# A two-layer diffusion transformer in fp32 on one core: order of the first loads and products, place of the modulations, order at phase borders

## The chip, the cores and the metric

The kernel runs on one core of a Trainium2 chip. The metric is the time of one execution on the device in microseconds (us). The engines named below are PE (TensorE, matrix products, with PEld for its weight loads), DVE (VectorE), ACT (ScalarE), POOL (GpSimd) and SP (SyncE, which issues the transfers, DMAs). Each engine takes its instructions in the order of the program; an instruction that waits holds everything behind it on its engine. All DMAs of this kernel are issued from SP's queue.

## What is computed

The input x holds 16 samples of 256 tokens with 256 features; cond is one vector of 256 features for each sample, ctx a context of 256 tokens with 192 features. Two layers follow each other, and each has three phases: self-attention, cross-attention on the context, and a feed-forward network (FFN). All is fp32.

```python
# layer 0: adaln(x) = ln(x, w, b) * (1 + cond @ g_w + g_b) + cond @ b_w + b_b
x = x + attn(adaln1(x), adaln1(x))            # 16 heads of 64, rotary positions
x = x + attn(adaln1(x), ln(ctx))              # the same modulation 1
x = x + gelu(adaln2(x) @ w1 + b1) @ w2 + b2
# layer 1: (sh1, sc1, sh2, sc2, sh3, sc3) = silu(cond) @ Wmod + bmod
x = x + attn(ln1(x) * (1 + sc1) + sh1) @ Wos + bos          # 16 heads of 16
x = x + attn(ln2(x) * (1 + sc2) + sh2, ctx) @ Woc + boc
x = x + gelu((ln3(x) * (1 + sc3) + sh3) @ W1 + b1) @ W2 + b2
```

## The kernel before

The program goes through the six phases one after the other, and in each phase through the 16 samples. A pair of phase and sample is a *job*; an attention job has two steps, an FFN job four. The loop over the list `steps` writes the work of all engines out in order: in the step of one job it also issues pieces of its neighbours (`prev`, `nxt`, `after`, `third` are the jobs one behind and one, two and three ahead). `tc.manual_schedule` keeps that order; before, it is entered only when the loads of phase 0 and the first modulation have been issued, and what stands ahead of it is ordered by the framework. The eight PSUM banks are given out by hand; in the FFN `next_bank()` goes round them.

*Products.* `product` (L82) makes four column tiles of 32 that run side by side. Each fp32 product is two PE instructions.

*Modulation.* `modulation` makes `factor` and `addend` for all samples of a phase from two 256x256 matrices: 8 products of 16 columns, so 16 PE instructions (L152), and on DVE four small operations for each half of the features (L158 to L161). Layer 0 has two modulations (the first also serves the cross-attention), layer 1 has three. `load_phase` loads a phase's modulation matrices (L139, L140) and weights while the first job of the phase before runs; the modulation itself is made in job 2 of the phase before.

*Attention input.* `prepare_moments` makes the statistics (DVE, and POOL for the power, L261), `prepare_norm` normalizes and turns blocks of 32 by 32 (DVE), writes them to HBM by four DMAs (`turned`, L284) and adds the output bias to x on POOL (`add_bias`, L354). `prepare_fetch` reads them back by four DMAs (`fetched`, L294), and `prepare_input` makes hT from them, one half on ACT (L327), one on POOL (L328). For the very first job PE makes the transposition instead (L803).

*Layer 0's attention.* `stage_rotary` makes queries and keys of two heads' halves, DVE multiplies them by the rotary table (L455), POOL adds or subtracts (qk, L463). `stage_s` makes the scores (L498) and ACT their exponentials (pr, L510). `stage_t`, `stage_turn` and `stage_reduce` sum them on DVE into `rows`; `layer0_values` (PE, then ACT copies, L407) makes the values, `layer0_sums` (L567) the weighted sums. `sum_up` takes the sums of a whole job with one small product, inverts them on DVE (L541), writes them to HBM and spreads them back by one and four DMAs (L544, L547). `scale` multiplies the weighted sums by them on POOL (L556, four operations). `finish` makes the output product and adds it to x on DVE (L704).

*Layer 1's attention.* `stage_a` makes queries and keys, `layer1_values` the values (DVE writes them, L418), `layer1_sums` the weighted sums (L583), `normalize` inverts (L609), shuffles and multiplies (DVE, POOL, L618).

*FFN.* `ffn_hidden` makes a quarter of the hidden features in a step, ACT applies gelu (L633). The second product is made in Strassen's way: `fold_weights` makes five sums of quarters of w2, `fold_hidden` five of the hidden features (both DVE), and `finish_folded` makes seven products of quarters and adds them to x by five DVE operations. The last job of a phase uses `finish` instead, which makes the whole product.

At the border from layer 0's cross-attention to the FFN, three of these chains end behind each other: the next-to-last job's `scale` and `finish`, and the last job's `sum_up`, `scale` and `finish`, which come in the FFN's first two jobs:

```python
                if s == 2 and prev["kind"] == "attn":
                    (sum_up if prev["layer"] == 0 else finish)(prev, next_bank())
                if late is not None and s == 0:
                    scale(late)
                if late is not None and s == 3:
                    finish(late, next_bank())
```

Of the kernel before, what the change touches and what calls it, by code (L numbers as in the profile page):

```python
# [10 lines left out]
F32 = mybir.dt.float32  # L11
# [5 lines left out]
P = 128  # L17
# [26 lines left out]
def fast(ctx: ExitStack, tc: tile.TileContext, a: dict, out: bass.AP, flag):  # L44
# [6 lines left out]
    assert NB >= 5  # L51
# [19 lines left out]
    turn_of_ffn = [0]  # L71
# [12 lines left out]

    ident = work.tile([P, P], F32, tag="ctx", name="ident")
# [36 lines left out]

    sig = work.tile([NB, D], F32, tag="inv", name="sig")
    nc.scalar.activation(sig, cond, AF.Sigmoid)
    silu = work.tile([NB, D], F32, tag="inv", name="silu")
    nc.vector.tensor_mul(silu, sig, cond)
    condT = const.tile([P, 2, KC, NB], F32, name="condT")
    pc = bank(5, 2 * KC, NB).rearrange("p (s c) b -> p s c b", s=2)
    for s, src in enumerate((cond, silu)):
        for c in range(KC):  # L130
            nc.tensor.transpose(pc[:, s, c, :], src[:, c * P : (c + 1) * P], ident[:NB, :NB])
    nc.vector.tensor_copy(condT, pc)
    pr = bank(6, n_rows)
    nc.tensor.transpose(pr, rows, ident[:n_rows, :n_rows])
    nc.vector.tensor_copy(cols, pr)
# [7 lines left out]
    def modulation(name, at, which, w, ln_w, ln_b, shift_b, scale_b):  # L143


        factor = stat.tile([P, KC, NB], F32, tag="fac", name=f"fac_{name}", bufs=3)
        addend = stat.tile([P, KC, NB], F32, tag="add", name=f"add_{name}", bufs=3)
# [8 lines left out]
        for m in range(KC):  # L156
            one = stat.tile([P, NB], F32, tag="one", name=f"one_{name}_{m}", bufs=2)
            nc.vector.tensor_scalar(one, pm[:, 1, m, :], scale_b(m), 1.0, ALU.add, ALU.add)  # L158
            nc.vector.tensor_scalar(factor[:, m, :], one, ln_w(m), None, ALU.mult)
            nc.vector.tensor_scalar(one, one, ln_b(m), None, ALU.mult)  # L160
            nc.vector.scalar_tensor_tensor(addend[:, m, :], pm[:, 0, m, :], shift_b(m), one, ALU.add, ALU.add)  # L161
        return factor, addend

    def layer0_modulation(i):
        w = load_modulation(a[f"L0_xcond_b{i}_w"], a[f"L0_xcond_g{i}_w"], f"a{i}")
        return lambda at: modulation(
            f"a{i}", at, 0, w,
            lambda m: column(f"L0_xcond_ln{i}_w", m), lambda m: column(f"L0_xcond_ln{i}_b", m),
            lambda m: column(f"L0_xcond_b{i}_b", m), lambda m: column(f"L0_xcond_g{i}_b", m),
        )  # L170

    def layer1_modulation(i):
# [4 lines left out]
        c = at // P  # L177
        return lambda at: modulation(
            f"b{i}", at, 1, w,
# [1366 lines left out]
```

## Time and profile before

| | us |
|---|---|
| three runs | 2239.78, 2242.82, 2244.06 (median 2242.82) |
| the profiled execution | 2240.03, its span 2238.2 |
| PE busy in the span | 2208.3 |
| DVE, ACT, POOL busy | 1583.4, 837.1, 866.2 |
| first product of a whole stage (values of job 0) | starts at 12.32 |
| last addition to x, then its DMA out | 2231.88, 2232.60 |

The phases stand in the span about like this: self-attention of layer 0 to 674, its cross-attention to 1309, its FFN to 1542, self-attention of layer 1 to 1776, its cross-attention to 2010, its FFN to the end. A row of the timeline gives start, time, engine, line, operation, what is written and read, how often, and in brackets how long the engine was idle before and what ended that. A row that says x32 covers 32 instructions from the start of the first to the end of the last. A row of the waits names the engine that waited, what it was to run, whom it waited for, and then the total, how often, and the longest. The engine called SPq is SP's queue.

### The profile page before, as it was taken

Reading aid. Unit: us, or ns where it says so; the run is one execution under the profiler, and the core shown is the slowest. Engines: PE = TensorE matmul, PEld = TensorE weight load, DVE = VectorE, ACT = ScalarE, POOL = GpSimd, SP = SyncE. Lnnn points to the kernel's source line nnn. Section 1 sums busy time; section 2 is a strip of 40 time slices with the busy share of each in tenths; the row PEclk is TensorE's granted clock in tenths of the full one; section 3 lists DMA queues with packets and bytes.
Section 4 is the critical chain, followed back from the end, with each engine's and each line's share of the span. In section 5 each row is a group of like instructions: output and inputs, shape, how many; then the busy total and the mean of one; then the engine's idle time right before and its main releaser. Section 6 shows DMA issues by size and latency. Waiting matters only on the chain.

```text
span 2238.2 us, 104439 instructions
## 1 busy us (share of the span) xinstructions
PE 2208.3 (99%) x47515; PEld 1365.8 (61%) x47515; DVE 1583.4 (71%) x3001; ACT 837.1 (37%) x1302; POOL 866.2 (39%) x873
## 2 busy tenths in 40 slices
PE   8999999999999999999999999999999999999998
PEld 4555555555555555555555557876566555656786
DVE  5777677677678787887878775564777777777663
ACT  2233233233233332333333232223666656663322
POOL 3444444444445455554554532211222322322220
PEclk9999999999999999999999999999999999999999
DMA  8111111011123221222212122222111232223221
GB/s 249 39 27 35 22 27 36 22 27 36 25 46 80 62 54 37 45 53 42 56 35 55 27 50 74 41 46 60 41 42 40 52 101 61 60 51 78 65 62 36
DMA packets 305678, 117.29 MB, mean 52 GB/s; under 512 B 242548, under 2 KB 288968, under 8 KB 305096
## 3 DMA queue, kind: packets, MB, share of 16 engines
q1 hardware_dynamic: 305224, 110.51, 20.7%
q8 instruction: 374, 6.13, 1.2%
q14 instruction: 80, 0.66, 0.1%
HBM read 77.14 MB, written 33.29 MB: 49 GB/s over the span
## 4 chain that ended last, share of the span: by engine, by line
PE 93%; DVE 2%; DMA 1%; POOL 1%; SPq 1%; issue 1%; ACT 0%; POOLq 0%; DVEq 0%; ACTq 0%
PE banks L82 60%; PE banks L498 15%; PE banks L567 9%; PE banks L583 5%; PE banks L434 2%; PE banks L402 1%; DMA wkv_sa<-in_sa_wkv 1%; POOL raw L556 0%; DVE m L455 0%; POOL qk L463 0%; DMA spread<-sums_seen 0%; SPq L284 0%; PE banks L152 0%; DMA every<-sums_seen 0%; DMA x<-in_x 0%
## 5 line engine op out<-in xcount | busy, mean ns | idle before, releaser
L510 ACT ACTIVATE pr<-banks 128x1024 f32<-128x1024 f32 x576 | 487.5, 937 | 222.8 <-PE banks L498 194.6
L463 POOL TENSOR_TENSOR qk<-m,m 128x512 f32<-128x512 f32 x256 | 340.9, 1352 | 341.0 <-DVE m L455 230.8
L455 DVE TENSOR_TENSOR m<-banks,rope 128x512 f32<-128x512 f32 x512 | 325.2, 681 | 92.8 <-POOL qk L463 57.2
L519 DVE TENSOR_TENSOR both<-pr 128x512 f32<-128x512 f32 x256 | 217.8, 860 | 72.7 <-ACT pr L510 70.6
L574 ACT COPY raw<-banks 128x512 f32<-128x512 f32 x128 | 75.0, 587 | 469.9 <-PE banks L567 389.3
L498 PE MATMUL banks<-qk 32*64 32x256 f32 x8192 | 238.5, 377 | 1.0 <-DVE inv L541 0.5
L567 PE MATMUL banks<-pr,v 128*32 128x256 f32 x4096 | 233.5, 379 | 1.5 <-ACT pr L510 1.2
L498 PEld LDWEIGHTS banks<-qk 32*64 32x64 f32 x8192 | 184.4, 131 | 78.4 <-issue 53.0
L633 ACT ACTIVATE g<-banks,cols 128x256 f32<-128x256 f32 x256 | 107.0, 472 | 283.4 <-PE banks L82 270.5
L407 ACT COPY v<-banks 128x512 f32<-128x512 f32 x128 | 71.9, 588 | 357.6 <-PE banks L82 178.9
L556 POOL TENSOR_TENSOR raw<-raw,spread 128x512 f32<-128x512 f32 x128 | 182.4, 1457 | 27.8 <-DMA spread<-sums_seen 27.3
L567 PEld LDWEIGHTS banks<-pr,v 128*32 128x32 f32 x4096 | 130.2, 110 | 84.7 <-ACT pr L510 1.7
L704 DVE TENSOR_TENSOR x<-banks,x 128x512 f32<-128x512 f32 x66 | 45.6, 691 | 165.8 <-PE banks L82 165.8
L525 DVE STREAM_TRANSPOSE squares<-both 128x1024 f32<-128x1024 f32 x128 | 159.1, 1243 | 3.3
L532 DVE TENSOR_REDUCE rows<-squares 128x32 f32<-128x1024 f32 x128 | 154.0, 1203 | 2.2
L261 POOL TENSOR_TENSOR rstd<-ve,neg_half 128x2 f32<-128x2 f32 x95 | 67.5, 710 | 205.8 <-DVE ve L259 202.4
L82 PE MATMUL banks<-hT,wkv_sa 128*32 128x256 f32 x2048 | 136.1, 380 | 0.0
L583 PE MATMUL banks<-pr,wide_v 128*32 128x256 f32 x2048 | 134.4, 379 | 1.1 <-ACT pr L510 1.1
L82 PE MATMUL banks<-hT,wq_sa 128*32 128x256 f32 x2048 | 135.1, 379 | 0.0
L82 PE MATMUL banks<-hT,wq_ca 128*32 128x256 f32 x2048 | 134.0, 379 | 0.0
L498 PE MATMUL banks<-q,k 32*64 32x256 f32 x4096 | 129.2, 382 | 2.5 <-DVE add_b L161 2.1
L618 POOL TENSOR_TENSOR oT<-oT,spread 128x256 f32<-128x256 f32 x64 | 45.8, 737 | 210.7 <-DVE spread L617 210.7
(142 smaller groups left out, 3473.0 us busy)
## 6 DMA issues: line engine op xcount, KB each, us to landing
turned<-blocks SPq DMA_DIRECT2D x380, 64.0 KB
fetched<-turned SPq DMA_DIRECT2D x380, 64.0 KB
spread<-sums_seen SPq DMA_DIRECT2D x128, 128.0 KB
x<-in_x SPq DMA_DIRECT2D x16, 256.0 KB
fetched_c<-turned_c SPq DMA_DIRECT2D x64, 64.0 KB
cT<-in_ctx_turned SPq DMA_DIRECT2D x16, 256.0 KB
out<-x SPq DMA_DIRECT2D x16, 256.0 KB
ctx<-in_ctx SPq DMA_DIRECT2D x16, 192.0 KB
```

The lines of the kernel that those rows point to most:

```text
L82: nc.tensor.matmul(out[cut], lhsT[:, cut], rhs, start=start, stop=stop)
L455: nc.vector.tensor_tensor(m, pq, rope[:, s : s + 1, :].to_broadcast([P, 2, N]), ALU.mult)
L463: nc.gpsimd.tensor_tensor(r, x, y, (ALU.subtract, ALU.add)[out])
L498: nc.tensor.matmul(banks[64 * g : 64 * g + 64, at + h, t * N : (t + 1) * N], lhs, rhs, start=(half == 0), stop=(half == 1 or job["layer"] ...
L510: nc.scalar.activation(pr[:, one], sc[:, one], AF.Exp, scale=0.125 if job["layer"] == 0 else 0.25)
L519: nc.vector.tensor_tensor(job["both"][:, 2 * p : 2 * p + 2, :], pr[:, :, 0, :], pr[:, :, 1, :], ALU.add)
L525: nc.vector.transpose(job["squares"].rearrange("p b k -> p (b k)"), job.pop("both").rearrange("p h n -> p (h n)"))
L532: nc.vector.tensor_reduce(job["rows"][:, u, :], job.pop("squares"), AX.X, ALU.add)
L556: nc.gpsimd.tensor_tensor(part, part, spread[:, u : u + 1, :].to_broadcast([P, 2, N]), ALU.mult)
L567: nc.tensor.matmul(o[32 * h : 32 * h + 32, half, :], v[:, t, col : col + 32], prs[h // 2][:, h % 2, t, :], start=(t == 0), stop=(t == NT - 1),
L583: nc.tensor.matmul(o[32 * h : 32 * h + 32], v[:, t, 4 * c + h, 32 * e : 32 * e + 32], prs[h // 2][:, h % 2, t, :], start=(t == 0), stop=(t ...
L633: nc.scalar.activation(g[:, c, :], ph[:, c, :], AF.Gelu, bias=column(w["b1"], 2 * u + c))
```

## The change

*The start.* The whole program now stands in the order in which it is written. The first loads go out in another order: behind the modulation's matrices come the first halves of keys' and queries' weights, rope, the values' weights, fold, mask and the next two samples, then the other halves, the bias and wo. Twenty idle products of 16 columns, whose result nobody reads, are put between the transpositions of cond, of silu and of the vectors, and behind them; a one-column Exp is put behind the Sigmoid. The first modulation is made ahead of the transposition of the normalized x. All four rotary pieces of job 0 come ahead of both value steps, and the preparations of jobs 1 and 2 are placed anew.

*Modulations.* `modulation` has five DVE operations over both halves instead of eight. The three modulations of layer 1 are loaded and made in layer 0's FFN, in its jobs 2, 5 and 8.

*Borders.* At the last step of layer 0's attention other banks are used for the sums and for `finish`. In layer 0's FFN `sum_up` moves one step ahead, `scale` from the second job's first step to the first job's last; in layer 1's FFN `finish` moves behind the hidden product; `fold_weights` moves from the fourth step to the second. The values of layer 1's first job get a bank for each half. At the last step of layer 1's attention `finish` goes ahead of the sums. The turn of the FFN's banks starts one later.

*The end.* The last job uses `fold_hidden` and `finish_folded` as well, with an order of its own and a third bank.

The diff, without changes of indentation; the quoted keys in `phases` and the passing of columns are left out:

```diff
-    turn_of_ffn = [0]
+    turn_of_ffn = [1]
...
+    ctx.enter_context(tc.manual_schedule(engines={
+        mybir.EngineType.PE, mybir.EngineType.DVE, mybir.EngineType.Activation, mybir.EngineType.Pool,
+        mybir.EngineType.SP,
+    }))
     ident = work.tile([P, P], F32, tag="ctx", name="ident")
...
+    def transpose_condition(s, src):
+        pc = bank(5 + s, KC, NB)
+        for c in range(KC):
+            nc.tensor.transpose(pc[:, c, :], src[:, c * P : (c + 1) * P], ident[:NB, :NB])
+        nc.vector.tensor_copy(condT[:, s], pc)
+
+    def idle_products(n):
+
+        for _ in range(n):
+            nc.tensor.matmul(bank(0, 16), ident, ident[:, 0:16], start=True, stop=True)
+
     nc.scalar.activation(sig, cond, AF.Sigmoid)
+    soon = stat.tile([NB, 1], F32, tag="ve", name="soon")
+    nc.scalar.activation(soon, cond[:, 0:1], AF.Exp)
     silu = work.tile([NB, D], F32, tag="inv", name="silu")
+    idle_products(5)
+    transpose_condition(0, cond)
     nc.vector.tensor_mul(silu, sig, cond)
-    for s, src in enumerate((cond, silu)):
-        for c in range(KC):
-            nc.tensor.transpose(pc[:, s, c, :], src[:, c * P : (c + 1) * P], ident[:NB, :NB])
-    nc.vector.tensor_copy(condT, pc)
-    pr = bank(6, n_rows)
+    idle_products(4)
+    transpose_condition(1, silu)
+    idle_products(5)
+    pr = bank(4, n_rows)
     nc.tensor.transpose(pr, rows, ident[:n_rows, :n_rows])
-    nc.vector.tensor_copy(cols, pr)
+    idle_products(6)
...
-        for m in range(KC):
-            one = stat.tile([P, NB], F32, tag="one", name=f"one_{name}_{m}", bufs=2)
-            nc.vector.tensor_scalar(one, pm[:, 1, m, :], scale_b(m), 1.0, ALU.add, ALU.add)
-            nc.vector.tensor_scalar(factor[:, m, :], one, ln_w(m), None, ALU.mult)
-            nc.vector.tensor_scalar(one, one, ln_b(m), None, ALU.mult)
-            nc.vector.scalar_tensor_tensor(addend[:, m, :], pm[:, 0, m, :], shift_b(m), one, ALU.add, ALU.add)
+        nc.vector.tensor_tensor(addend, pm[:, 1], scale_b, ALU.add)
+        nc.vector.scalar_tensor_tensor(factor, addend, 1.0, ln_w, ALU.add, ALU.mult)
+        nc.vector.scalar_tensor_tensor(addend, addend, 1.0, ln_b, ALU.add, ALU.mult)
+        nc.vector.tensor_tensor(addend, addend, shift_b, ALU.add)
+        nc.vector.tensor_tensor(addend, pm[:, 0], addend, ALU.add)
...
+        load_keys(halves[0])
+        load_queries(halves[0])
+        if between is not None:
+            between(0)
+        load_keys(halves[2])
+        load_keys(halves[3])
+        if between is not None:
+            between(1)
+        load_queries(halves[1])
+        load_keys(halves[1])
+        bo = broadcast_row(a[f"L0_xcond_{kind}_bo"], "bo", f"bo_{kind}")
         nc.sync.dma_start(out=wo, in_=chunked(a[f"{kind}_wo"]))
...
+        if job is jobs[-1]:
+            sums = sums[4:] + sums[:4]
...
+        third = bank(next_bank(), 4, P) if final else second
...
+        for m in (3, 6, 4, 5, 2, 1, 7) if final else places:
             for c in range(4):
-                product(place, hidden[m][:, c, :], weights[m][:, c, :], c == 0, c == 3)
+                product(places[m], hidden[m][:, c, :], weights[m][:, c, :], c == 0, c == 3)
...
-    for dst, name in ((rope, "rope"), (fold, "fold"), (mask, "mask")):
-        nc.sync.dma_start(out=dst, in_=a[name])
-    for b in range(1, NB):
+    for b in range(3, NB):
         load_x(b)
-    phases[0]["mod"] = phases[0]["make_mod"](4)
...
-    xh = normalized(xs[0], moments(xs[0], "first"), D, "first")
+    found = moments(xs[0], "first")
+    nc.vector.tensor_copy(cols, pr)
+    xh = normalized(xs[0], found, D, "first")
+    phases[0]["mod"] = phases[0]["make_mod"](3)
...
     prepare_input(jobs[0])
-    add_bias(jobs[0])
-    layer0_values(jobs[0], 0)
     for e in range(2):
         for half in range(2):
             rotary((jobs[0], 0), e, half)
-    layer0_values(jobs[0], 1)
+        if e == 0:
+            prepare_moments(jobs[1])
+    for t in range(NT):
+        layer0_values(jobs[0], t)
     scores(0)
-    for job in jobs[1:3]:
-        prepare_moments(job)
-        prepare_norm(job)
+    prepare_norm(jobs[1])
     prepare_fetch(jobs[1])
+    add_bias(jobs[0])
+    prepare_moments(jobs[2])
+    prepare_norm(jobs[2])
     prepare_input(jobs[1])
...
+        if ffn and layer0 and job["b"] in (2, 5, 8):
+            at = phases[3 + job["b"] // 3]
+            if s == 0:
+                at["make_mod"] = at["mod_load"]()
+            if s == 3:
+                make_mod = at
...
-            if s == 2 and prev["kind"] == "attn":
-                (sum_up if prev["layer"] == 0 else finish)(prev, next_bank())
+            if s == 1 and prev["kind"] == "attn" and layer0:
+                sum_up(prev, next_bank())
             ffn_hidden(job, s)
+            if s == 2 and prev["kind"] == "attn" and not layer0:
+                finish(prev, next_bank())
             if prev["kind"] == "ffn":
...
-            elif s == 3:
-                fold_weights(job["phase"])
...
-            if late is not None and s == 0:
-                scale(late)
...
             if s == 2 and then:
-                at = next_bank()
                 for t in range(NT):
-                    layer1_values(then[0], at, t)
+                    layer1_values(then[0], next_bank(), t)
...
+            if s == 1 and prev["kind"] == "attn":
+                fold_weights(job["phase"])
             if s == 3 and after is not None:
                 prepare_input(after)
+            if s == 3 and prev["kind"] == "attn" and layer0:
+                scale(prev)
...
-                sum_up(late, 0)
+                sum_up(late, 0 if nxt["kind"] == "attn" else 6)
...
-                layer0_sums(job, 2 * s + e, 4 + e)
+                layer0_sums(job, 2 * s + e, 4 + e if then else e)
...
-                finish(late, 1)
+                finish(late, 1 if then else 7)
...
+            for e in range(2) if not then else []:
+                finish(prev, at + 1, (e,))
             for e in range(2):
                 layer1_sums(job, s, e, at + 2 + e)
-                if s == 1:
+                if s == 1 and then:
                     finish(prev, at + 1, (e,))
...
-            if make_mod:
-                make_mod["mod"] = make_mod["make_mod"](at)
...
-    finish(jobs[-1], next_bank())
+    fold_hidden(jobs[-1])
+    finish_folded(jobs[-1])
```

## The prediction

> **What bounds the kernel now.** First the page: span, busy shares, slices.
>
> ```profile
> span 2238.2 us, 104439 instructions
> PE 2208.3 (99%) x47515; PEld 1365.8 (61%) x47515; DVE 1583.4 (71%) x3001; ACT 837.1 (37%) x1302; POOL 866.2 (39%) x873
> PE   8999999999999999999999999999999999999998
> ```
>
> TensorE (PE) bounds every stage; only its first and last slices are not full. No part removes products, apart from some at the end. So I list what PE waits for, then read the timeline around each wait. PE's waits, whole run:
>
> ```profile
> PE banks L82 <- POOL raw L556: 4.2, 7, 2.5
> PE banks L82 <- ACT hT L327: 2.7, 2, 1.6
> PE banks L498 <- DVE add_b L161: 2.1, 2, 1.0
> PE banks L82 <- POOL oT L618: 1.6, 1, 1.6
> PE banks L82 <- DVE wide_v L418: 0.7, 1, 0.7
> ```
>
> All lie at the start or at phase borders: some 20 us to be had, no more. Timelines of the start (PE, then SP's queue, POOL, DVE):
>
> ```profile
> 7.07 3.46 PE L152 MATMUL banks<-condT,mod_a 128*128 128x16 f32 x16
> 12.32 5.70 PE L82 MATMUL banks<-wkv_sa,hT 128*32 128x512 f32 x32 [1.08 <-ACT hT L327]
> 24.76 3.60 PE L82 MATMUL banks<-wkv_sa,hT 128*32 128x512 f32 x32
> 44.63 3.64 PE L82 MATMUL banks<-wkv_sa,hT 128*32 128x512 f32 x32 [1.60 <-ACT hT L327]
> 8.09 6.12 SPq L190 DMA_DIRECT2D bo_sa<-in_L_xcond_sa_bo  x1
> ```
>
> The same 32 products take 5.70 us at 12.32 and 3.60 at 24.76: the weight loads beside them step by 0.85 us until 16.56 and by 0.43 after. PE runs at half rate until 16.5. The borders and the end:
>
> ```profile
> 1303.36 0.35 DVE L541 RECIPROCAL inv<-banks 128x32 f32<-128x32 f32 x1
> 1310.85 5.89 POOL L556 TENSOR_TENSOR raw<-raw,spread 128x512 f32<-128x512 f32 x4 [1.29 <-DMA spread<-sums_seen]
> 1322.13 3.66 PE L82 MATMUL banks<-hT,w_a 128*32 128x256 f32 x64 [0.81 <-DVE x L704]
> 1343.54 4.96 POOL L556 TENSOR_TENSOR raw<-raw,spread 128x512 f32<-128x512 f32 x4 [7.30 <-DMA spread<-sums_seen]
> 1344.85 1.07 PE L82 MATMUL banks<-wo_ca,raw 128*32 128x256 f32 x16 [2.52 <-POOL raw L556]
> 1595.86 1.12 PE L498 MATMUL banks<-q,k 32*64 32x256 f32 x32 [1.04 <-DVE add_b L161]
> 2231.88 0.69 DVE L704 TENSOR_TENSOR x<-banks,x 128x512 f32<-128x512 f32 x1 [7.82 <-PE banks L82]
> ```
>
> The sum is made against the profiled execution, 2240.03 us (span 2238.2 plus 1.8 around it), 2.8 below the median 2242.82 of the three runs.
>
> **1. Start.** Twenty idle products make 40 PE instructions in front of the first modulation, at 0.213 each at half rate (3.46/16; PE is there bound by the loading of 128 columns) or 0.112 at full rate (later modulations: 16 in 1.79). ident is there at 1.4. At half rate all through: 10 idle to 3.5, cond's transposes to 3.9, 8 to 5.6, silu's to 6.0, 10 to 8.1, rows to 8.4, 12 to 11.0, modulation to 14.4, xh's transposes to 15.3; five DVE operations (0.23 plus gaps, 1.3 in all; before, four stood ahead of the first hT) and hT's 0.6 give first dense products at 16.5, against 12.32. With the switch at 5.6 (4.2 us after the first product, what the dense stretch 12.32 to 16.5 took): modulation done by 10.3, dense products at 12.3. The new DVE order (condT, silu, condT before x0's statistics, then cols before xh) has xh by 9.7 at worst, before PE asks.
>
> Behind the first dense product comes less waiting. Rotary pairs (6.92 us), two value steps (6.92), scores: 13.9 us from first product to scores at full rate, before 15.97. POOL's qk, for which scores waited 0.5 in all, has 6.9 us of values as cover. The first wait of job 1 (1.76 over its normal step) goes: fetched is issued straight behind turned of job 1, no longer behind that of job 2; I put it at 38 us (the loads drain at 33; turned, then fetched, some 2.5 each), needed at 40.7. Then the 0.45 at 51.2. Gain at 12.3: 2.1+0.5+1.76+0.45=4.8. At 16.5 half rate lasts into the products as before: 2.7-4.2=-1.5.
>
> On SP's queue rope, fold, mask, x1, x2 move ahead of wq's and wk's second halves, bo ahead of wo; the bytes ahead of the first values are 3.2 MB, drained by 13 us at the rate of the windows (2.8 MB at 12); needed at 19. x1 is needed at 17. add_bias(0) moves behind qk on POOL, which no longer waits 15 us for bo. The Exp table load (1.28 at 29.04) moves to about 3; it lay beside scores. Nothing from that.
>
> Does the rate switch before the dense products? The nearest row in kind says no: from 6.8 to 11.2 PE ran the same light products, and still ran at half rate. But that was 4.4 us, hardly more than the 4.2 that dense ones needed, and 1.1 us of idle followed; the new stretch has 9 us without a stop. I take a switch near 7, first dense product at 13.0: 4.1; ends -1.5 and 4.8.
>
> The Trainium skill, "TensorE: Matmul & The Clock Gate", Part 1, says that hardware watches a free-running window of about 3.4 us and doesn't count instructions. By it the switch comes 3.4 to 6.8 us after the first idle product, dense products at 12.3 to 13.7, and the start gains 3.4 to 4.8. By the row above it would lose 1.5. This trace doesn't show light products releasing the clock.
>
> **2. Modulation code, five DVE operations for eight.** Only at 805.9 (0.47 over the step: layer0_sums waits for the bank) is it on the path: 3 operations of 0.27 less, 0.3; ends 0 and 0.5.
>
> **3. Cross-attention into FFN.** The last steps use other banks, so sums need not wait 1.2 us, nor scores 0.54; both only move into finish's wait for POOL's scale, which is pinned by the reciprocal at 1303.36 and the DMA behind it (1310.85): nothing. The first hidden step has another bank than finish: 0.81, at 1321.2. sum_up now stands ahead of hidden 1: it waits for rows, reduced on DVE until 1324.5, 1.5 us in which hidden 1 stands behind it. In return its reciprocal comes at 1326 instead of 1329.15; its five DMAs pass the four fetches (hT of job 2 goes from 1334.7 to 1337, needed at 1350); scale's four go on POOL from 1343.5 to about 1338.4, behind that hT. finish then doesn't wait (2.52+3x0.16) and ends at 1350.0, not 1352.89: 2.9. fold_weights (5x0.68 on DVE) moves ahead, beside hidden products; if they didn't cover it, 3.4. fold_hidden still follows it at 1332.6. Ends: -0.7 (the rows' wait without the gain) and 3.5.
>
> **4. FFN into layer 1.** Values get a bank each: wide_v's wait (0.73+0.16) goes: 0.9. The 0.38 and 0.43 behind belong to ACT's chain gelu, table, exp, which starts 0.9 earlier too. Ends 0 and 1.3.
>
> **5. Layer 1's modulations.** Two leave attention steps in which scores waited 1.20 each over their pace: 2.4. In the FFN they stand as the one at 1364 did, which no PE wait follows. Their two loads a time go on SP's queue ahead of the fetches, 0.9 us, and 512 KB; hT has 7.6 us of slack there (made at 1360.3, used at 1367.9). Low end 1.0: the 0.47 of point 2 each time.
>
> **6. Layer 1 into FFN.** finish ahead of the last sums waits for POOL's oT (2014.8), some 1.1 us longer than exps were waited for; finish behind hidden 2 saves the 1.61. About 0.2; ends -0.8 and 1.6.
>
> **7. End.** The direct finish (7.1 us of PE) becomes seven folded products of a quarter's size, 6.12 (as at 2216.78 to 2222.90). The first needs no sum, the second's is made from early halves; the other sums (0.64 each) run from 2225.8 ahead of their products. PE ends at 2230.8, and one addition of 0.42 remains for 0.69: 1.3. If sums come late, nothing; ends 0 and 1.3.
>
> **Sum:** 4.1+0.3+2.9+0.9+2.4+0.2+1.3=12.1; 2227.9 against the profiled execution, 2230.7 beside the median.
>
> **Rivals.** A, the forecast. B: light products don't release the clock. For it speaks the half rate after 11.2; against it the longer stretch. Start -1.5: gain 6.5, 2236.3. C: the switch comes, but point 3 gives -0.7, since scale or its DMAs are late again (each of spread's landings took 5 us from its first issue): gain 8.5, 2234.3. D: B and C together: gain 2.9, 2239.9. E, slower: a modulation load holds SP's queue, as bo did for 6.12 us at 8.09 and its like for 4.97 at 47.9, and fetches stand behind it. Below 7.6 us a hold is free. The three must hold 13.2 each to eat 12.1 and 4.6 more (3x5.6): 2247.4. The loads at 1340.7 took 0.40 and 0.47, which speaks against it.
>
> **How the numbers follow.** This kernel's measurement tells about 0.2%, 4.5 us. Chances: A 0.50 (its own range 2227.4 to 2233.5), B 0.22, C 0.12, D 0.08, E 0.08. A and C are faster; B is 2 us beyond the bound, 0.16 faster and 0.06 same; D same. So faster 0.78, same 0.14, slower 0.08. The range leaves out D and E: from 2226.5 (all upper ends together, 3.3 more, and 0.9 for the runs' scatter) to 2238.5 (B without points 4 and 7).
>
> **What would show it.** Weight loads in the first rotaries stepping by 0.43 or 0.85; first dense product at 12.3 to 13.7 or 16.5; no wait for hT near 40; sum_up waiting some 1.5 for rows, no long wait for raw after it; no add_b among PE's waits; last DVE addition of 0.42. Wrong it is if a dense stretch runs at half rate for longer, if SP holds, or if a border's wait only moves on.

## The result, and the profile after

| | before | after |
|---|---|---|
| median of nine runs each, us | 2241.86 (2238.92 to 2244.06) | 2237.38 (2233.29 to 2239.39) |
| profiled execution, its span | 2240.03, 2238.2 | 2237.38, 2235.6 |

The ratio is 0.9978, with a 95% interval of 0.9968 to 0.9989: faster by 4.5 us between the medians, 2.65 between the two profiled executions. The forecast was 12.1 (2230.7). A second series, told below as the run of the changed kernel again, gave 0.9972 (0.9962 to 0.9982).

The busy times of the engines on the page of the changed kernel (PEld are PE's weight loads):

```profile
PE 2215.1 (99%) x47651; PEld 1384.8 (62%) x47651; DVE 1579.1 (71%) x2996; ACT 836.7 (37%) x1303; POOL 865.9 (39%) x873
```

PE is busy for 6.8 us more in a span that is 2.6 shorter. The forty instructions of the idle products, at 0.213 each, are 8.5 of it. The waits of PE in the changed kernel, in the form used before (engine, what it was to run, releaser: total, times, longest):

```profile
PE banks L82 <- DVE folded L699: 3.7, 1, 3.7
PE banks L82 <- POOL raw L585: 2.4, 4, 2.0
PE banks L82 <- POOL oT L647: 1.8, 1, 1.8
PE banks L82 <- ACT pr L539: 1.5, 2, 1.3
PE banks L82 <- DVE rows L561: 1.4, 1, 1.4
PE banks L82 <- ACT hT L356: 0.9, 1, 0.9
```

Those for add_b, x and wide_v are gone, and of hT's 2.7 the 0.9 in front of the very first product is left. The largest one, 3.7 for `folded` (the sums of hidden features; 0.88 before), stands in layer 1's FFN, where the forecast looked at nothing. The timeline of the changed kernel at the start:

```profile
1.35 2.31 PE L139 MATMUL banks<-ident 128*128 128x16 f32 x10 [1.35 <-POOL ones L95]
8.35 2.68 PE L139 MATMUL banks<-ident 128*128 128x16 f32 x12
10.87 3.57 PE L171 MATMUL banks<-condT,mod_a 128*128 128x16 f32 x16
16.29 1.93 PE L82 MATMUL banks<-hT,wkv_sa 128*32 128x256 f32 x16 [0.92 <-ACT hT L356]
18.00 1.72 PE L82 MATMUL banks<-hT,wq_sa 128*32 128x256 f32 x16
19.55 1.04 PE L82 MATMUL banks<-hT,wkv_sa 128*32 128x256 f32 x16
```

The modulation's 16 instructions still take 3.57 at 10.87, after 9 us of idle products without a stop. The first 16 dense instructions take 1.93, those at 19.55 take 1.04. The half rate ends at 19.37, where the trace has its first record of full clock (before: 16.52). The light products released nothing.

The timeline of the changed kernel at the borders and the end (PE, POOL, DVE). `every` is a copy of all collected sums of the attention, which DVE reduces once, in layer 1's FFN:

```profile
1325.27 0.22 PE L82 MATMUL banks<-fold,rows 128*32 128x32 f32 x1 [1.44 <-DVE rows L561]
1339.35 5.00 POOL L585 TENSOR_TENSOR raw<-raw,spread 128x512 f32<-128x512 f32 x4
1343.50 7.13 PE L82 MATMUL banks<-wo_ca,raw 128*32 128x256 f32 x128
2004.21 2.22 PE L527 MATMUL banks<-q,k 32*64 32x256 f32 x64
2008.28 3.17 PE L82 MATMUL banks<-wo_b,oT 128*32 128x256 f32 x32 [1.85 <-POOL oT L647]
2021.19 7.09 PE L82 MATMUL banks<-hT,w_b 128*32 128x256 f32 x128
2034.54 2.29 DVE L748 TENSOR_REDUCE worst<-every 128x1 f32<-128x2048 f32 x1 [5.09 <-DMA every<-sums_seen]
2045.52 1.95 PE L82 MATMUL banks<-w_b,folded 128*32 128x128 f32 x64 [3.66 <-DVE folded L699]
2229.51 0.42 DVE L720 TENSOR_TENSOR x<-banks,x 128x256 f32<-128x256 f32 x1
```

`finish` at 1343.50 waits for nothing any more. But at 2008.28 PE waits for oT, and its 32 instructions take 3.17 instead of some 2.2. A window of the changed kernel says why (stretch, length, busy time of PE, PEld, DVE, ACT and POOL, then the granted clock of PE, the DMA share and GB/s):

```profile
2009.00:2012.00 3.00, 3.00 (x32) 1.55 (x36) 0.44 (x1) 0.28 (x1) 0.70 (x1) 0.56 0.01 4
```

The granted clock fell to half for 3.41 us, from 2009.35 to 2012.76. In windows at the start that column shows 1.00, since no record stands there; the half rate of the start is read from the pace of the products.

Of before, these rows of the timeline stand against them:

```profile
67.20 3.06 PE L498 MATMUL banks<-qk 32*64 32x256 f32 x104
2010.08 2.22 PE L498 MATMUL banks<-q,k 32*64 32x256 f32 x64
2036.47 2.29 DVE L716 TENSOR_REDUCE worst<-every 128x1 f32<-128x2048 f32 x1 [4.30 <-DMA every<-sums_seen]
2047.47 1.95 PE L82 MATMUL banks<-w_b,folded 128*32 128x128 f32 x64 [0.88 <-DVE folded L667]
```

The same places in both traces, in the order of time. Each gain is the change of the difference between two neighbouring rows:

| up to | before | after | gain | forecast |
|---|---|---|---|---|
| scores of job 1 of phase 0 | 67.20 | 67.54 | -0.34 | +4.1 |
| first `finish` products behind the cross-attention's modulation | 807.64 | 807.47 | +0.51 | +0.3 |
| last step of layer 0's attention | 1299.67 | 1299.78 | -0.28 | 0 |
| first hidden product behind the late `finish` | 1352.89 | 1350.40 | +2.60 | +2.9 |
| first scores of layer 1, less 3.78 for two modulations more in the FFN | 1541.70 | 1542.36 | +0.63 | +0.9 |
| last scores of layer 1, with these 3.78 given back | 2010.08 | 2004.21 | +2.75 | +2.4 |
| last hidden quarter of the FFN's first job | 2026.00 | 2021.19 | -1.06 | +0.2 |
| first folded products behind it, in the next job | 2047.47 | 2045.52 | -2.86 | 0 |
| end of the last addition | 2232.57 | 2229.93 | +0.69 | +1.3 |
| sum | | | +2.64 | +12.1 |

(3.78 is twice 1.89, the distance from the modulation at 1363.57 to the products behind it.) Three rows hold 8.6 of the 9.5 us that are missing: the start 4.4, the border from layer 1's attention into the FFN 1.3, and the next job's folded products 2.9.

### The profile page after: what moved, and what is told of

It is laid out like the page before. It is cut to its first block, busy times and chain, and to the rows that moved or that the text cites. A ratio compares the mean times of both kernels' runs of the same rounds, so it can differ in the third digit from the quotient of the medians.

```text
span 2235.6 us, 104704 instructions
## 1 busy us (share of the span) xinstructions
PE 2215.1 (99%) x47651; PEld 1384.8 (62%) x47651; DVE 1579.1 (71%) x2996; ACT 836.7 (37%) x1303; POOL 865.9 (39%) x873
## 4 chain that ended last, share of the span: by engine, by line
PE 97%; DVE 1%; POOL 1%; issue 0%; DMA 0%; SPq 0%; ACT 0%; DVEq 0%; POOLq 0%; ACTq 0%
PE banks L82 63%; PE banks L527 16%; PE banks L596 10%; PE banks L612 5%; PE banks L463 1%; PE banks L431 1%; PE banks L171 0%; PE banks L139 0%; DMA every<-sums_seen 0%; POOL raw L585 0%; POOL qk L492 0%; DVE m L484 0%; DVE sums L638 0%; SPq L323 0%; SPq L313 0%
## 5 line engine op out<-in xcount | busy, mean ns | idle before, releaser
L548 DVE TENSOR_TENSOR both<-pr 128x512 f32<-128x512 f32 x256 | 210.8, 831 | 77.3 <-ACT pr L539 75.6
```

The source lines that it names most:

```text
L548: nc.vector.tensor_tensor(job["both"][:, 2 * p : 2 * p + 2, :], pr[:, :, 0, :], pr[:, :, 1, :], ALU.add)
```

## The experiments

The theory: the light idle products delay the first dense ones and do not release the clock; in layer 1 the waits that were taken away only moved, to POOL's oT and to DVE, which stands behind a DMA. The second half of it held only in part, as the second execution of the changed kernel and the modulations alone show. The rivals stand with each run. Times are medians, ratios are to the kernel before on the same chip.

**The changed kernel without idle products.**

```diff
-    idle_products(5)
     transpose_condition(0, cond)
     nc.vector.tensor_mul(silu, sig, cond)
-    idle_products(4)
     transpose_condition(1, silu)
-    idle_products(5)
...
-    idle_products(6)
```

> The changed kernel without its twenty idle products; all else as changed. Theory 1 (the idle products only delay: they are too light to release the clock): the first dense product comes at about 11.7 us instead of 16.29, PE still runs at half rate for some 4 us from there, and the whole is about 4 us faster than the changed kernel (ratio to before near 0.996). Theory 2 (they do bring the release forward, only late): without them the half rate lasts until about 19 us or longer, and no more than 2 us are gained over the changed kernel (ratio 0.997 or above).

Measured: 2229.55 (2229.03 to 2232.19), ratio 0.9946 (0.9932 to 0.9959). Its timeline:

```profile
5.80 3.59 PE L167 MATMUL banks<-condT,mod_a 128*128 128x16 f32 x16 [1.13 <-DMA mod_a<-in_L_xcond_b_w]
11.25 1.94 PE L82 MATMUL banks<-hT,wkv_sa 128*32 128x256 f32 x16 [0.92 <-ACT hT L352]
15.76 1.04 PE L82 MATMUL banks<-hT,wq_sa 128*32 128x256 f32 x16
63.06 3.71 PE L523 MATMUL banks<-qk 32*64 32x256 f32 x128
2037.75 1.95 PE L82 MATMUL banks<-w_b,folded 128*32 128x128 f32 x64 [2.40 <-DVE folded L695]
```

Dense products begin 5.0 us earlier, and the clock is released at 15.13, 3.9 behind the first of them. The scores of job 1 stand at 63.06 instead of 67.54. So the new order of the loads and products is worth 4.1 us against before (67.20), about what was forecast for the whole start (though by other terms, see the point on the start), and the idle products took all of it away. The gain over the changed kernel is 7.8 in the profiled pair, about twice what theory 1 expected; the part that is not the start's 4.5 comes later: here the wait for oT costs no clock, and the one for `folded` is 2.40.

**The changed kernel with idle products of 512 columns: 2, 1, none and 1 of them.**

```diff
-            nc.tensor.matmul(bank(0, 16), ident, ident[:, 0:16], start=True, stop=True)
+            nc.tensor.matmul(
+                bank(0, 4, P), ident, ident.unsqueeze(1).to_broadcast([P, 4, P]), start=True, stop=True
+            )
...
-    idle_products(5)
+    idle_products(2)
```

> The changed kernel with four idle products of 512 columns (2, 1, 0 and 1 at the four places) for the twenty of 16 columns. Theory 1 (what releases the clock is how densely the columns stream, not how long PE has instructions): weight loads step at full rate by 8.3 us at the latest, the first dense product comes near 12.5 us and runs at full rate, and the whole is about 5 us faster than the changed kernel (ratio to before near 0.9955). Theory 2 (only a product with real work ahead, or a longer stretch, releases it; light modulation products close it again): the first dense product comes near 14.5 us or later and runs at half rate, about 1.5 us faster than the changed kernel (ratio 0.997).

Measured: 2231.88 (2229.36 to 2232.82), ratio 0.9948 (0.9935 to 0.9962). Its timeline and, below, its windows:

```profile
7.26 1.85 PE L172 MATMUL banks<-condT,mod_a 128*128 128x16 f32 x16
10.97 1.79 PE L82 MATMUL banks<-hT,wkv_sa 128*32 128x256 f32 x16 [1.12 <-ACT hT L357]
12.51 1.95 PE L82 MATMUL banks<-hT,wq_sa 128*32 128x256 f32 x16
```

```profile
11.00:14.00 3.00, 3.00 (x32) 1.53 (x36) 0.49 (x1) 0.00 (x0) 0.00 (x0) 0.53 1.08 367
2004.00:2008.00 4.00, 3.94 (x44) 1.63 (x40) 1.01 (x4) 0.83 (x1) 1.18 (x2) 0.57 0.01 3
```

Wide idle products release the clock: full from 4.35, 3.0 behind the first of them, and the modulation takes 1.85 instead of 3.57. But 2.6 us of light products (the modulation and the transpositions) and a wait of 1.12 follow, and at 11.18 the clock falls to half for 3.41 us, just as the dense products begin. So it is what the products stream that releases the clock, and not that PE has something to do. The scores of job 1 stand at 63.92, 0.9 behind the run without idle products; what was won on the modulation was lost again. Each theory is half right: the clock was released as theory 1 said and lost as theory 2 said. The ratio is near theory 1's 0.9955, but the run without idle products has the same one, so it shows nothing for wide idle products. Whether the light products or the wait lost the clock, this run can't tell. It also lost the clock at 2004.56, behind the wait for oT.

**The changed kernel with the two reductions over `every` in the next two jobs instead of behind its DMA.**

```diff
+    def sum_outside():
+        worst, every = checked[0]
         nc.vector.tensor_reduce(worst[:, 0:1], every, AX.X, ALU.add)
...
-        if job["last"] and s == 0 and job["b"] in (1, 4):
-            (look_outside if job["b"] == 1 else count_outside)()
+        if job["last"] and s == 0 and job["b"] in (1, 2, 3, 4):
+            (look_outside, sum_outside, least_outside, count_outside)[job["b"] - 1]()
```

> The changed kernel, with the two reductions over the collected sums (DVE, 2.3 us each, which wait for the DMA of every) put into the last FFN's jobs 2 and 3, while the DMA stays where it is. Theory 1 (PE's 3.66 us wait at 2045.5 comes from DVE standing behind that DMA, the same point that pinned the kernel before): the wait falls below 0.7 us, no later wait takes its place, gain about 3 us over the changed kernel (ratio to before near 0.9965). Theory 2 (the wait comes from the weights' sums being made earlier, or DVE is simply full there): the wait stays above 2.5 us or comes back in jobs 2 and 3, gain under 1 us.

Measured: 2232.79 (2232.34 to 2234.66), ratio 0.9961 (0.9947 to 0.9974), 4.6 under the changed kernel's 2237.38 and 2.5 under the 2235.32 of its second series. Its timeline:

```profile
2007.74 2.19 PE L82 MATMUL banks<-wo_b,oT 128*32 128x256 f32 x32 [1.85 <-POOL oT L647]
2018.96 7.09 PE L82 MATMUL banks<-hT,w_b 128*32 128x256 f32 x128
2031.64 2.05 PE L82 MATMUL banks<-folded_w,folded 128*32 128x128 f32 x67 [1.25 <-issue]
2040.34 2.01 PE L82 MATMUL banks<-w_b,folded 128*32 128x128 f32 x62
```

There is no wait for `folded` left: from the last hidden quarter to the folded products it is 21.38 instead of 24.33, though 1.25 of another wait, which the profile puts down to nothing (the last section says what it is), stands between. This shows where the wait for `folded` comes from: DVE takes its instructions in order, and behind the reductions that wait for the DMA stand the sums of hidden features that PE needs. In the changed kernel the reductions begin 13.35 behind the last hidden quarter (2021.19 to 2034.54), before 10.47 (2026.00 to 2036.47). Some 1.3 of it is a later issue of the DMA (6.15 behind that quarter instead of 4.86), 1.6 a longer way from issue to reduction (7.20 instead of 5.61). The same wait for oT as in the changed kernel, 1.85, cost no clock here.

**The changed kernel with the old place of `finish` in layer 1's last attention step.**

```diff
-            for e in range(2) if not then else []:
-                finish(prev, at + 1, (e,))
             for e in range(2):
                 layer1_sums(job, s, e, at + 2 + e)
-                if s == 1 and then:
+                if s == 1:
                     finish(prev, at + 1, (e,))
```

> The changed kernel, with layer 1's last attention step as before: output product between the weighted sums, not ahead of them. Theory 1 (the output product ahead of the sums only lengthens the wait for POOL, and that wait let the clock fall to half for one stretch of 3.41 us): the wait near 2007 falls from 1.85 to about 1.1, no half-rate record there, and PE reaches the fourth hidden step of the next phase's first job 1.0 to 2.0 us earlier; the long wait near 2045 grows by as much, so the whole time is the same within 1 us. Theory 2 (the clock falls on its own there): the half-rate record stays, and nothing but some 0.3 us is gained.

Measured: 2235.16 (2233.15 to 2237.63), ratio 0.9969 (0.9958 to 0.998); its interval and the changed kernel's overlap, so the times alone say little. Its timeline does:

```profile
1313.91 8.37 PE L82 MATMUL banks<-wo_ca,raw 128*32 128x256 f32 x120 [2.08 <-POOL raw L585]
2004.88 2.22 PE L527 MATMUL banks<-q,k 32*64 32x256 f32 x64
2008.17 1.07 PE L612 MATMUL banks<-pr,wide_v 128*32 128x256 f32 x16 [1.07 <-ACT pr L539]
2011.83 5.36 PE L82 MATMUL banks<-hT,w_b 128*32 128x256 f32 x96
```

From the last scores to the FFN's first hidden product it takes 6.95 (before 6.94), in the changed kernel 9.49, and with the new order and the full clock, in the runs without idle products and with spread reductions, 7.8. So the new place of `finish` costs 0.85 by the wait alone, and 1.7 more when the clock is lost behind it. What it gives back is the wait of 1.61 for oT in front of the FFN's first `finish`, of which 0.12 is left: net 0.6 won with the full clock, 1.1 lost without it. In this run the clock was lost elsewhere, at 1314.36, behind a wait of 2.08 for POOL's raw. The wait for `folded`, which theory 1 had growing, is 0.91 here, with 1.71 put down to nothing in front of it.

**The changed kernel again**, unchanged, in a second profiled execution.

> The changed kernel as it is, a second profiled execution. Theory 1 (the order decides: the wait for POOL's oT and the one for DVE's folded are set by the program): the same waits at the same places, 1.85 +- 0.1 at the last step of layer 1's attention and 3.6 +- 0.2 on folded in the next phase, first dense products at 16.3; time 2235 to 2239. Theory 2 (the half-rate stretch of 3.41 us behind the wait for oT depends on where that wait falls in windows that run on by themselves): it may be missing or stand elsewhere in this execution; the step from the last scores of the attention to the first hidden products then takes about 8 us and not 9.5, and the time is about 1.4 shorter.

Measured: 2235.32 (2232.54 to 2239.73), ratio 0.9972 (0.9962 to 0.9982), the profiled execution 2234.74. Its timeline and its windows:

```profile
2008.98 2.20 PE L82 MATMUL banks<-wo_b,oT 128*32 128x256 f32 x32 [1.84 <-POOL oT L647]
2033.21 2.05 PE L82 MATMUL banks<-folded_w,folded 128*32 128x128 f32 x67 [1.56 <-issue]
2042.63 1.95 PE L82 MATMUL banks<-w_b,folded 128*32 128x128 f32 x64 [0.35 <-DVE folded L699]
```

```profile
2009.00:2013.00 4.00, 3.94 (x72) 2.18 (x76) 1.69 (x6) 1.88 (x4) 1.32 (x2) 1.00 0.02 6
```

The wait for oT is the same, 1.84, so the order sets it. The half rate behind it is not there: the step takes 7.8 and not 9.49, so theory 2 holds for the clock. Against theory 1 the wait for `folded` is 0.35, with 1.56 put down to nothing in front of it; together 1.91, where the first execution had 3.83. The DMA took 5.58 from its issue to the reduction here, 7.20 there. So 1.9 of the 2.86 belongs to that one execution, and in the row above it (-1.06) the 1.7 of the lost clock: here that row reads +0.63.

All nine rows of the table read -1.17, 0.51, -0.28, 2.71, 0.63, 2.76, 0.63, -0.95 and 0.70 in this execution, 5.5 in all. Of the 6.6 us that are missing from the forecast here, the start holds 5.3: the clock was released at 21.33, 5.0 behind the first dense product instead of 3.1. The next job's folded products are the other term that loses in both executions.

**The kernel before with only the modulations changed**: five operations, and layer 1's loaded and made in layer 0's FFN.

```diff
+            if ffn and layer0 and job["b"] in (2, 5, 8):
+                at = phases[3 + job["b"] // 3]
+                if s == 0:
+                    at["make_mod"] = at["mod_load"]()
+                if s == 3:
+                    make_mod = at
```

> The kernel before with only the modulation in five operations and layer 1's three modulations loaded and made in layer 0's FFN. Theory 1 (these two points of the change are worth what their waits were): no wait for add_b is left, layer 1's two attention phases are 6.2 us shorter together (3.8 of products that move into the FFN, 2.4 of waits), the FFN 3.8 longer, the wait of 0.47 at 805.9 is gone; 2.7 us faster than before, 2239. Rival (the DMA that spreads every is pinned, so that what layer 1's attention saves is waited for on folded): the wait for folded in the last FFN grows from 0.9 to 1.5 or more, and the gain is under 1.5 us, 2240.5.

Measured: 2237.92 (2236.37 to 2240.96), ratio 0.9981 (0.9972 to 0.999). Its timeline:

```profile
1344.55 7.64 PE L82 MATMUL banks<-wo_ca,raw 128*32 128x256 f32 x92 [3.85 <-POOL raw L555]
2008.49 2.22 PE L497 MATMUL banks<-q,k 32*64 32x256 f32 x64
2046.15 1.96 PE L82 MATMUL banks<-w_b,folded 128*32 128x128 f32 x64 [1.30 <-DVE folded L666]
```

From the first hidden product behind the late `finish` (1353.96, before 1352.89) to layer 1's last scores it gains 2.66, which is theory 1's number; the wait for `folded` grows by 0.42 only, so the rival falls. The whole change has 0.9978 and 0.9972: by these ratios the start, the borders and the end added 0.7 to 2.0 us to the modulations, which lies inside the intervals. The run also shows how a border takes a gain away. It came to job 1's scores 1.33 earlier than before (65.87), with its clock released at 14.99. In front of the late `finish` the wait for POOL's raw then grew from 2.52 to 3.85, by just that, and from 1342.77 on the clock was at half for 6.83 us.

**Three edits together**: no idle products, reductions spread, old place of `finish`.

> The changed kernel without idle products, with the reductions of the next-to-last job spread over two later jobs as in e3, and with the old order of finish in the last step of layer 1's attention as in e4. Theory 1 (the three add up): from e1's 2229.6 the wait for folded (2.4 there) goes and the wait in layer 1's last step falls from 1.84 to about 1.1: 2226.0 to 2227. Rival (waits only move on: a third one takes their place, as waits that the profile puts down to nothing did in e3 and e4, 1.3 to 1.7 each): 2228 to 2229.5.

Measured: 2227.92 (2227.65 to 2229.16), ratio 0.9937 (0.9924 to 0.995). Between the two expectations, 0.1 from the rival's: 1.6 under the run without idle products alone. Its waits:

```profile
PE banks L82 <- issue: 2.5, 2, 1.6
```

Those for `folded` and oT (2.40 and 1.84) are gone, 1.07 for exponentials is back, and what the profile puts down to nothing has grown from 0.33 to 2.5. The last section says what these waits are. One (0.94) stands at 51.9, behind the loads of the next phase's weights, the other (1.59) at 2028.25, 7 us behind the issue of the DMA of `every`.

**The same with wide idle products**, and two more between the transposition of the normalized x and the first dense products.

```diff
+    idle_products(2)
     transpose_condition(0, cond)
     nc.vector.tensor_mul(silu, sig, cond)
+    idle_products(1)
     transpose_condition(1, silu)
...
+    idle_products(2)
     prepare_input(jobs[0])
```

> v1, but with e2's idle products of 512 columns, and two more of them between the transposition of the normalized x and the first dense products. Theory 1 (the clock is kept by streaming columns): it is released near 4.4 and stays, first dense products near 11 at full rate, against 11.2 at half rate until 15 in v1: 1.5 to 2 us faster than v1. Rival (the light modulation between them is enough to lose it again, as in e2 at 11.2): half rate for 3.4 us from near 11, and no faster than v1 by more than 0.5 us.

Measured: 2226.45 (2226.02 to 2229.35), ratio 0.9932 (0.9919 to 0.9945): 1.5 under the run above, theory 1's number, and 16.2 us under before on the same chip. Its timeline:

```profile
7.75 1.85 PE L172 MATMUL banks<-condT,mod_a 128*128 128x16 f32 x16
10.18 1.88 PE L139 MATMUL banks<-ident 128*128 128x512 f32 x4
11.99 1.07 PE L82 MATMUL banks<-hT,wkv_sa 128*32 128x256 f32 x16
```

The clock is full from 5.55 until PE has done its last product (2217.77; the record of half clock behind it begins at 2220.80): the dense products begin at 11.99, later than without idle products (11.47), but at 1.07 for 16. Job 1's scores stand at 62.23, 2.0 before those of the run above. This is the lowest median of the kernels here.

**That kernel with the old order at the border into layer 0's FFN** (the sums' product a step later, `scale` in the second job).

```diff
-            if s == 1 and prev["kind"] == "attn" and layer0:
+            if s == 2 and prev["kind"] == "attn" and layer0:
                 sum_up(prev, next_bank())
...
+            if late is not None and s == 0:
+                scale(late)
...
-            if s == 3 and prev["kind"] == "attn" and layer0:
-                scale(prev)
```

> v2 with the old order at the border into layer 0's FFN: the sums' product one step later, scale in the second job's first step. Theory 1 (point 3 of the change is worth its 2.6): the wait of 1.44 for rows goes, a wait of 3.5 to 4.5 for POOL's raw stands in front of the late finish, and from the first hidden product of the FFN (1315.94 in v2) to the first one behind that finish (1344.48) it takes 31 us instead of 28.5: 2228.5 to 2229.5. Rival (the wait also loses the clock for a stretch of 3.41 us or more, as in the run with the modulations alone): 1.4 to 2.8 longer still, 2230 to 2232. Rival 2 (later waits give it back): no more than 1 us over v2's 2226.4.

Measured: 2229.98 (2228.24 to 2230.39), 3.5 over the run above, which ran on another chip (4.3 by the ratios); ratio 0.9951 (0.9937 to 0.9964). Its timeline:

```profile
1340.00 1.07 PE L82 MATMUL banks<-wo_ca,raw 128*32 128x256 f32 x16 [3.07 <-POOL raw L586]
1348.04 5.36 PE L82 MATMUL banks<-hT,w_a 128*32 128x256 f32 x96
```

From the FFN's first hidden product (1316.37) to the one at 1348.04 it takes 31.67 instead of 28.54: point 3 of the change is worth 3.1 here. In the profiled pair 1.5 of it comes back at 2028, where a wait that the profile puts down to nothing is 0.19 instead of 1.67; that wait varies from execution to execution. Even so the profiled pair differs by 2.1, more than rival 2 allows. The wait of 3.07 lost no clock in the profiled execution, so the first rival is not seen there.

**That kernel with the old end**, the last product made whole.

```diff
-    fold_hidden(jobs[-1])
-    finish_folded(jobs[-1])
+    finish(jobs[-1], next_bank())
```

> v2 with the old end: the last job's second product made whole, one addition of 512 columns behind it. Theory 1 (point 7 of the change, 0.8 in the pair of traces): the products behind the last hidden quarter take 7.0 instead of 6.2 with the sums ahead of them, and the last addition 0.65 instead of 0.42; 0.8 to 1.0 longer, 2227.3. Rival (the two ends are the same within their waits): 2226.4.

Measured: 2227.3 (2224.95 to 2227.99), 0.85 over the 2226.45 measured on another chip (1.1 by the ratios), within the runs' scatter; the trace decides. From the last hidden quarter (2210.01) to the end of the last addition (2218.99 and 0.69) it takes 9.67, with the new end 8.98: 0.69, the same as between before and after.

## Why the prediction was right or wrong, point by point

The direction and the range were right, the size was not: of the forecast's 12.1, 2.6 is in the profiled pair and 4.5 between the medians.

**1, the start: wrong, and the step is named.** "I take a switch near 7, first dense product at 13.0" failed; rival B happened, with its first dense product at 16.29 (B: 16.5), because the light products here did not release the clock. The prediction had the row that said so, modulation and transposes at half rate from 6.8 to 11.2, and set it aside as too short. The estimate from the Trainium skill ("TensorE: Matmul & The Clock Gate", Part 1), dense products at 12.3 to 13.7, missed as well. The page counts from what is issued first ("Whatever you issue in your first ~3.4 µs runs at 1.2 GHz; everything after runs at 2.4 GHz"); here 14 us of idle products, transpositions and modulation (1.35 to 15.37) ran at half rate. B's own price, -1.5, came out at -0.34 and, in the second execution, at -1.17; the two differ by how far behind the first dense product the clock was released (3.1 and 5.0; B had 4.2). Without idle products the start is worth 4.1, the forecast's own number, but that is luck: dense products 1.07 earlier, the clock 0.3 sooner behind them (worth half of that), and some 2.9 of waits gone (the forecast had 2.7 of these), in place of an early clock.

**2 and 5, the modulations: right.** The wait at 805.9 is gone, 0.51 (forecast 0.3). Layer 1's attention gains 2.75 beyond the products moved (forecast 2.4), and the kernel with only these edits shows 2.66. The loads held nothing on SP's queue (rival E): the six in the FFN took 0.48 to 0.62 each to issue.

**3, the entry into the FFN: right.** The wait for rows is 1.44 (forecast 1.5), `scale` starts at 1339.35 (1338.4), `finish` waits for nothing; 2.60 for 2.9 in the pair, 3.1 in the better kernel. Rival C, the late `scale`, didn't come.

**4 and 7: right in kind, smaller.** The wait for wide_v is gone, but the one for exponentials behind it grew to 1.29 at 1545.79: 0.63 for 0.9. The end: 0.69 for 1.3. What was mis-sized is the last addition: from the last hidden quarter to the last product it takes 8.03 instead of 8.82 (forecast 7.9), but behind the last product stand two additions of 0.42, at 2228.98 and 2229.51, and not one.

**6, layer 1's attention into the FFN: wrong, -1.06 for 0.2.** The wait, 0.8 longer than that for exponentials, was in the forecast at 1.1. Not in it was that a wait of 1.85 can put the clock at half for 3.41 us (1.7 us of work). With the full clock it gains 0.6, as the second execution shows.

**What was missing: layer 1's FFN, -2.86.** No step of the forecast went behind hidden 2 of its first job. There the waits of before had the sign of it, one for `folded` of 0.88, behind reductions that wait 4.30 for a DMA. The forecast put this stretch at nothing; 0.95 of loss shows in the second execution too, the other 1.9 came with a DMA of 7.20 in the first. The chain hangs on its DMA, not on the hidden products: the 0.6 that PE won just ahead of it at full clock is waited for behind it. What was won further ahead is not, since the issue of the DMA moves with the program: it comes 20.8 us behind layer 1's last scores before, 20.7 with the modulations alone, which keep their 2.66 and wait 0.42 longer, and 21.1 in the second execution. The change also moves `fold_weights` ahead of the reductions; in the trace DVE only waits longer there (5.09 for 4.30), but no run moved it alone. The closing sentence of the forecast named the kind ("if a border's wait only moves on"), with no place and no price.

## What to carry to other kernels

Filler products that are to release the matrix engine's clock must be wide: here 512 columns did it and 16 did not, and nothing between was tried. Test them by the pace of the first real products, and if those come later than without fillers, take the fillers out. When waits are taken away ahead of a chain that hangs on a DMA, follow every queue to the next place where that chain is waited for, and move the waiting instruction behind the work that others need. A wait's price is not its length alone: it may cost the clock behind it, in some executions and not in others.

## What the runs showed of the hardware that I had not expected

*What releases the clock.* Where light products or none run ahead of the dense ones, the trace's first record of full clock comes 2.7 to 5.0 us behind the first dense product (before 4.2, after 3.1, modulations only 2.7, without idle products 3.9, the changed kernel again 5.0), however long light products ran ahead. With 512-column idle products it comes 2.9 to 5.4 us behind the first of those (four profiles). Weight loads are no measure of it: a light product loads the same 128 columns of weights as a wide one.

*When it is lost.* All changes of the clock within one execution lie a whole number of 3.413 us apart (in the changed kernel 1989.97 us, 583 times, from the release to the loss at 2009.35). The loss comes with a wait, but not with every wait: it came with waits of 1.85 (the changed kernel and that with wide idle products), 2.08, 1.12 with light products ahead of it, and, for two periods, 3.85; it did not come with 1.84, 1.85 and 1.84 at the very same place in three other runs, nor with 1.95 at 1313.82 in the changed kernel, 2.52 (before), 3.07, and the longest of the changed kernel, 3.66 for `folded`. That fits a window whose place is set by the time of the release and not by the program. Laid in steps of 3.413 from the release, the window that ended at 2009.35 held 1.90 of idle PE; in the second execution the same wait is cut into 0.75 and 1.15. Idle time is not the whole rule: five windows with 1.90 to 2.04 of it kept the clock, in five profiles. The Trainium skill's window of about 3.4 us ("TensorE: Matmul & The Clock Gate", Part 1) agrees with these records in its length.

*What it makes of the scatter.* Of the 18 timed executions of the changed kernel, the eight with a mean granted clock of 0.999 took 2232.5 to 2237.0 us, the ten with 0.998 or 0.997 took 2235.3 to 2239.7. The kernel with wide idle products and moved waits, which keeps the clock from 5.55 on, had 0.999 or 1.0 in all five. So had the runs without idle products and with spread reductions, which keep the wait for oT, so this alone doesn't show that the moved waits keep the clock.

*Waits put down to nothing.* PE waits that the profile ascribes to no engine stand in most of the runs 5 to 8 us behind the issue of the DMA of `every`, between the same products and not always at the same length (0.27 before, 0.17 and 1.56 in two executions of the changed kernel, up to 1.7 in others); five profiles have another near 50 us, of 0.50 to 1.83. The traces say what they are. The page lists a queue for instructions (packets, MB, share of the DMA engines):

```profile
q8 instruction: 374, 6.13, 1.1%
```

That is one packet of 16 KB for each 255 of PE's 95302 products and weight loads. Each of the 16 waits ends 1.26 to 1.55 us behind the end of such a packet, however long the wait was, and the product behind it stands in the 194th or 195th place of a run of 256 PE instructions, in all eleven profiles that have such a wait. At none of the some 370 such places of a profile does PE go on earlier than 1.25 us behind the end of the packet that belongs there. So PE waits there for its own instructions, at the same few places of the program, until their packet is there. Why the packet is late is open; no run moved it.
